# Attention values of a Macaron block: full 512-column matmuls against 256-column passes with 64-row key blocks

## The chip, the cores and the metric

The kernel runs on one core of one Trainium2 chip. The metric is the device time in microseconds (us) of one launch. All data are float32.

## The reference

```
x = x + 0.5 * ffn(layernorm(x));  x = x + attn(layernorm(x));  x = x + 0.5 * ffn(layernorm(x))
ffn:   base = x @ W_base.T + b_base
       plus, with weights w from a top-2 softmax router over 8 experts, 2 * sum_e w_e * (x @ A_e.T) @ B_e.T   (rank 16)
attn:  q = rope(x @ wq) (32 heads of 128), k = rope(x @ wk), v = x @ wv (8 heads of 128), S = 256
       allowed = (j <= i) & (j > i - 128)             # a causal window of 128 keys
       out = softmax(q k^T / sqrt(128), allowed) @ v;  return out @ wo
```

The input x is 4 sequences of 256 tokens, each of width 512.

## The kernel before

The tokens are handled in two halves `h` of two sequences each. A **group** `(h, g)` is one key head `g` with its 4 query heads, and a **unit** `(h, g, b)` is one group on one sequence `b` of the half: 16 groups, 32 units. Units go in order, two to a group (`b` = 0, then `b` = 1).

For each unit the loop at L708 writes this work, one unit ahead where it can: keys (L374) and value projections (L465, tile `pv`) for a later group; `normalize` (L524, GpSimd) of this unit's probabilities; the output products of the *previous* unit (`outputs`, L581, tile `y`), which wait in the queue `late`; where `b` is 0, the queries of the next group (L400); `transposes` (L533, L537, L542); `scores` of the next unit (L482 `sa`, L497 `sb`); `values` (L553 to L561) of this unit; and the exponentials of the next unit (L515, ScalarE). ScalarE and GpSimd keep the order in which the loop writes their work. The order on TensorE and VectorE is the scheduler's.

**Blocks of keys.** The 256 queries of a head are four blocks of 64. The first two need only keys 0 to 127. Each of the last two needs three key blocks of 64, but of the first and the last of the three a query uses complementary triangles only. `scores` therefore folds these two into one block (L502), so that the probabilities of every pair of blocks are 128 x 128. After the transposition, where rows are keys, `transposes` parts the folded block again: it multiplies once by the mask `old` and once by `new` (L542), which gives `p1 = [old_p, new_p]`. Each has the third query block in columns 0 to 255 (`e` = 0: 4 heads x 64 queries) and the fourth in columns 256 to 511 (`e` = 1). `old_p` is multiplied with the values of keys 0 to 127 (`va` in the diff), `new_p` with those of keys 128 to 255 (`vb`). In the third block, `new_p` is zero in rows 64 to 127; in the fourth, `old_p` is zero in rows 0 to 63.

**`values` before.** The bank `oa` takes one matmul of 512 columns: `p0`, the first two query blocks, with the values of keys 0 to 127. The bank `ob` takes two: `old_p` and `new_p`, added up. A float32 matmul is two weight loads and two passes in the profile, so this is 6 passes of 512 columns a unit. ScalarE copies each bank to the tile `oT` as it is finished: `oa` to the first 128 tokens, `ob` to the last 128.

**After `values`.** `outputs` multiplies `oT` with the output weights by a scheme with 7 products instead of 8. It needs four sums and differences of the quarters of `oT`, made on GpSimd (`sums_a`, L114; tile `oTs`). Their order is: first minus second 128 tokens of heads 0 and 1; for the last 128 tokens, heads 0 and 1 plus heads 2 and 3; then `s2`; then `s4`. The products come in the order 4, then 1 and 6, then 2 and 3, then 7 and 5. Product 4 and product 1 take quarters of `oT` as they are. Product 6 takes `s2`, which is the third GpSimd instruction.

All matmul banks (`mm_bank`) come from one pool of four PSUM banks.

Of the kernel before, what the change touches and what calls it, by code (L numbers as in the profile page):

```python
# [17 lines left out]
P = 128  # L18
# [4 lines left out]
G = NH // NKV  # L23
# [6 lines left out]
BLK = 64  # L30
# [7 lines left out]
def macaron_kernel(  # L38
# [15 lines left out]
    nc = tc.nc  # L54
# [5 lines left out]
    def mm_bank(name):  # L60
        return ps.tile([P, 512], F32, tag="mm", bufs=4, name=name)
# [466 lines left out]
    def transposes(h, g, b, pr):  # L528
        def turn(n0, name):
            pt = ps.tile([P, 2, G, BLK], F32, tag="s", bufs=4, name=f"{name}_{h}_{g}_{b}")  # L530
            for p in range(G // 2):
                for e in range(2):
                    nc.tensor.transpose(pt[:, e, 2 * p : 2 * p + 2, :], pr[:, n0 + 2 * p + e, :], ident)  # L533
            return pt

        p0 = sb.tile([P, 2, G, BLK], F32, tag="p0", bufs=1, name=f"p0_{h}_{g}_{b}")
        nc.scalar.copy(p0, turn(0, "t0"))  # L537
        pt = turn(G, "t1")
        parts = []
        for n, w in enumerate((old, new)):  # L540
            part = sb.tile([P, 2, G, BLK], F32, tag=f"p1{n}", bufs=1, name=f"p1{n}_{h}_{g}_{b}")
            nc.vector.tensor_tensor(  # L542
                part, pt, w.unsqueeze(2).to_broadcast([P, 2, G, BLK]), ALU.mult
            )
            parts.append(part)
        return p0, parts

    def values(h, g, b, p0, p1):
        oT = sb.tile([HD, G, S], F32, tag="oT", bufs=4, name=f"oT_{h}_{g}_{b}")
        v = vS[h, g - g % 2]  # L550
        cols = ts(g % 2, HD)
        for i, parts in enumerate(([p0], p1)):
            po = mm_bank(f"o{'ab'[i]}_{h}_{g}_{b}")  # L553
            for n, part in enumerate(parts):
                nc.tensor.matmul(  # L555
                    po, v[:, 2 * b + n, cols], part, start=(n == 0), stop=(n == len(parts) - 1)
                )
            nc.scalar.copy(  # L558
                oT[:, :, ts(i, P)].rearrange("p j (e q) -> p e j q", e=2),
                po.rearrange("p (e j q) -> p e j q", e=2, j=G),  # L560
            )  # L561
        return oT

# [144 lines left out]
    for u, (h, g, b) in enumerate(units):  # L708
        n = groups.index((h, g)) + 1
# [26 lines left out]
        p0, p1 = transposes(h, g, b, ahead[0])  # L736
# [5 lines left out]
        if left > 1:  # L742
            ahead = scores(*units[u + 1])
        oT = values(h, g, b, p0, p1)
        if left > 1:
            exponentials(*ahead)
# [67 lines left out]
```

## Time and profile before

| what | value |
|---|---|
| median of 3 runs | 792.85 us (792.47 to 793.61) |
| the profiled execution's own time | 793.98 us |
| its span, first to last instruction | 792.3 us |
| TensorE (PE) busy | 780.0 us, 98% of the span |
| share of PE in the chain that ended last | 96% |
| VectorE (DVE), ScalarE (ACT), GpSimd (POOL) busy | 61%, 28%, 57% |
| granted TensorE clock | 1.000 |

PE is the matmuls and PEld the weight loads, which have rows of their own. A matmul's row gives the time from its start to the end of its result; neighbours overlap, so the cost of one in a row of many is the distance from start to start, which the timeline gives. A merged line of the timeline (x8) stands for several instructions of one kind; the next line's start tells how long they held the engine. In brackets stands the time that the engine sat idle before a line, and what released it.

### The profile page before, as it was taken

To read this page: it belongs to the slowest core of one execution; us is meant where nothing else is said; L and a number is where in the kernel's file an instruction comes from. 1 tells how busy PE (TensorE), PEld (TensorE's weight loads), DVE (VectorE), ACT (ScalarE), POOL (GpSimd) and SP (SyncE) were. 2 spreads that over 40 slices of the span, in tenths; PEclk is the share of its full clock that TensorE was granted. 3 is DMA by queue.
4 is the path that set the end of the run, shared out by engine and by line. 5 is a ranking of instruction groups with operands and counts; after the bars stand their busy time and mean duration, and the time that the engine had idled before them with its cause. 6 is when DMAs were issued, how large, how long until landed. Compare 5 with 4: busy or idle time off the path is not lost.

```text
span 792.3 us, 10145 instructions
## 1 busy us (share of the span) xinstructions
PE 780.0 (98%) x3524; PEld 602.6 (76%) x3524; DVE 486.6 (61%) x1226; ACT 222.1 (28%) x766; POOL 451.4 (57%) x461
## 2 busy tenths in 40 slices
PE   6999999999999999999999999999999999999998
PEld 4557878787878888787878787878788787877654
DVE  4558563838474756659487728484757557574663
ACT  4342333222213140312222232213141412223331
POOL 5421775674747474757575665747474756653521
PEclk9999999999999999999999999999999999999999
DMA  8400221212021302112121212020303021100001
GB/s 294 158 1 19 76 67 53 93 54 67 8 99 41 106 14 91 57 53 67 54 95 53 67 54 88 23 95 9 106 14 101 20 58 49 54 1 26 1 27 54
DMA packets 33555, 48.90 MB, mean 62 GB/s; under 512 B 1248, under 2 KB 14304, under 8 KB 33504
## 3 DMA queue, kind: packets, MB, share of 16 engines
q1 hardware_dynamic: 33504, 48.26, 18.6%
q8 instruction: 28, 0.46, 0.2%
q14 instruction: 23, 0.19, 0.1%
HBM read 46.15 MB, written 2.10 MB: 61 GB/s over the span
## 4 chain that ended last, share of the span: by engine, by line
PE 96%; DMA 1%; DVE 1%; ACT 1%; SPq 0%; POOL 0%; issue 0%; DVEq 0%; ACTq 0%
PE q L400 24%; PE y L581 23%; PE pv L465 7%; PE ob L555 7%; PE pp_k L374 7%; PE po_f L330 6%; PE sb L497 5%; PE sa L482 4%; PE t L533 4%; PE oa L555 3%; PE pa_f L317 2%; PE po_f L342 1%; DMA x<-in_x_dram 1%; PE y L620 1%; PE pt_f L246 1%; ACT probs L515 0%
## 5 line engine op out<-in xcount | busy, mean ns | idle before, releaser
L369 POOL TENSOR_TENSOR qT<-ra_q,rb_q 128x512 f32<-128x512 f32 x64 | 81.4, 1272 | 154.9 <-DVE rb_q L365 154.9
L581 PE MATMUL y<-wo,oT 128*128 128x256 f32 x368 | 94.8, 379 | 0.0
L365 DVE TENSOR_TENSOR rb_q<-q,sin_sb 64x512 f32<-64x512 f32 x128 | 88.1, 688 | 1.7
L597 DVE TENSOR_TENSOR x<-y,x 128x256 f32<-128x256 f32 (+1 forms) x62 | 34.0, 548 | 83.0 <-PE y L581 82.9
L114 POOL TENSOR_TENSOR oTs<-oT 128x256 f32<-128x256 f32 x62 | 45.8, 738 | 59.7 <-ACT oT L558 57.2
L581 PEld LDWEIGHTS y<-wo,oT 128*128 128x128 f32 x368 | 69.8, 190 | 9.4
L537 ACT COPY p<-t 128x512 f32<-128x512 f32 x32 | 18.8, 586 | 203.1 <-PE t L533 203.1
L524 POOL TENSOR_TENSOR probs<-probs,sm 128x512 f32<-128x512 f32 x64 | 66.2, 1055 | 1.2 <-DVE sm L519 1.2
L581 PE MATMUL y<-wos,oTs 128*128 128x256 f32 x248 | 63.9, 380 | 0.6 <-POOL oTs L114 0.6
L465 PEld LDWEIGHTS pv<-wv,xa 128*128 128x128 f32 x256 | 48.6, 190 | 18.1 <-issue 12.9
L400 PE MATMUL q<-xa,wq 128*128 128x256 f32 x256 | 60.8, 379 | 0.0
L400 PE MATMUL q<-xs,wqs 128*128 128x256 f32 x256 | 60.6, 379 | 0.0
L400 PE MATMUL q<-xs,wq 128*128 128x256 f32 x256 | 60.5, 379 | 0.0
L555 PE MATMUL ob<-p,v 128*128 128x512 f32 x128 | 60.1, 592 | 0.0
L465 PE MATMUL pv<-wv,xa 128*128 128x256 f32 x256 | 60.0, 379 | 0.0
L330 PE MATMUL po_f<-wb_sb,xn_f 128*128 128x512 f32 x128 | 57.9, 594 | 0.0
L374 PE MATMUL pp_k<-xa,wk 128*128 128x512 f32 x128 | 57.5, 592 | 0.0
L590 DVE TENSOR_TENSOR z<-y,z 128x512 f32<-128x512 f32 x46 | 31.7, 690 | 40.2 <-PE y L581 40.2
L515 ACT ACTIVATE probs<-probs,nm 128x64 f32<-128x64 f32 (+1 forms) x128 | 46.3, 364 | 35.7 <-DVE nm L511 30.2
L400 PEld LDWEIGHTS q<-xa,wq 128*128 128x128 f32 x256 | 48.5, 190 | 6.9 <-issue 0.2
L400 PEld LDWEIGHTS q<-xs,wqs 128*128 128x128 f32 x256 | 48.6, 190 | 6.6
L581 PEld LDWEIGHTS y<-wos,oTs 128*128 128x128 f32 x248 | 46.9, 190 | 7.5 <-POOL oTs L114 1.0
(142 smaller groups left out, 1489.2 us busy)
## 6 DMA issues: line engine op xcount, KB each, us to landing
wq<-in_wq_dram SPq DMA_DIRECT2D x16, 1024.0 KB, 5.4
wo<-in_wo_dram SPq DMA_DIRECT2D x16, 1024.0 KB, 5.3
wk<-in_wk_dram SPq DMA_DIRECT2D x16, 256.0 KB, 2.7
wv<-in_wv_dram SPq DMA_DIRECT2D x8, 512.0 KB, 3.5
x<-in_x_dram SPq DMA_DIRECT2D x8, 256.0 KB, 7.2
out_dram<-x SPq DMA_DIRECT2D x8, 256.0 KB, 2.0
wb_sb<-in_w_base_dram SPq DMA_DIRECT2D x1, 1024.0 KB, 7.8
ar_sb<-in_w_ar_dram SPq DMA_DIRECT2D x1, 272.0 KB, 4.8
```

Source lines behind the costliest of these rows:

```text
L114: nc.gpsimd.tensor_tensor(dst, p, q, op)
L330: nc.tensor.matmul(po[i], x_of(i, c), wb_sb[:, c, :], start=(c == 0), stop=False)
L365: nc.vector.tensor_tensor(twice(b[o : o + half, :]), twice(src[i : i + half, :]), angle(sin_sb[o : o + half, :]), ALU.mult,)
L369: nc.gpsimd.tensor_tensor(dst, view(a), view(b), ALU.add)
L374: nc.tensor.matmul(pp, w[:, c, :], xa[h][:, c, :], start=(c == 0), stop=(c == KC - 1))
L400: nc.tensor.matmul(bank[:, ts(j, S)], w[:, c, ts(j, HD)], x[:, c, :], start=(new and j == 0 and c == 0), stop=(c == 1), skip_group_check=True,
L465: nc.tensor.matmul(pv[:, : 2 * HD], xa[h][:, c, ts(i, P)], weights["v", h, g][:, c, :], start=(c == 0), stop=(c == KC - 1),)
L497: nc.tensor.matmul(pb[:, ts(e, 3 * BLK)], q[:, 2 + e, 2 * p : 2 * p + 2, :], k[:, n - P : n + BLK], start=True, stop=True,)
L515: nc.scalar.activation(pr[:, n, :keys_of], src[:, :keys_of], AF.Exp, bias=nm[:, n : n + 1], scale=scale, accum_out=sm[:, n : n + 1],)
L524: nc.gpsimd.tensor_tensor(w, w, sm[:, n : n + G].unsqueeze(2).to_broadcast([P, G, P]), ALU.mult)
L555: nc.tensor.matmul(po, v[:, 2 * b + n, cols], part, start=(n == 0), stop=(n == len(parts) - 1))
L581: nc.tensor.matmul(py[:, ts(i, D // 2)], lhs[n - 1][:, c, :], weights["os", h, g][n - 1][:, c, :], start=(i == 0 and c == 0), stop=(c == 1 ...
```

## The change

Only `values` is changed. Two banks are open at once. The bank of index `e` holds, in columns 0 to 255, the first (`e` = 0) or second (`e` = 1) query block, and in columns 256 to 511 the third or fourth.

- Four matmuls of 128 rows and 256 columns: `p0` of each block with `va`, then `old_p` of the third block with `va` and `new_p` of the fourth with `vb`.
- Four matmuls of 64 rows and 128 columns for what is left: `new_p` of the third block in rows 0 to 63 into bank 0, and `old_p` of the fourth block in rows 64 to 127 into bank 1. Each is cut in two by columns, and the two row groups take turns.
- Then the two copies to `oT`. Each bank now holds 64 of every 128 tokens, so each copy writes to both halves of the tokens, and each of the quarters that `sums_a` reads comes from both copies.

```
         cols = ts(g % 2, HD)
-        for i, parts in enumerate(([p0], p1)):
-            po = mm_bank(f"o{'ab'[i]}_{h}_{g}_{b}")
-            for n, part in enumerate(parts):
+        old_p, new_p = p1
+        va, vb = (v[:, 2 * b + n, cols] for n in range(2))
+        banks = [mm_bank(f"o{n}_{h}_{g}_{b}").rearrange("p (e c) -> p e c", e=2) for n in "ab"]
+        def block(t, e):
+            return t[:, e, :, :].rearrange("p j q -> p (j q)")
+        for e in range(2):
+            nc.tensor.matmul(banks[e][:, 0, :], va, block(p0, e), start=True, stop=True)
+        nc.tensor.matmul(
+            banks[0][:, 1, :], va, block(old_p, 0), start=False, stop=False, skip_group_check=True
+        )
+        nc.tensor.matmul(
+            banks[1][:, 1, :], vb, block(new_p, 1), start=False, stop=False, skip_group_check=True
+        )
+        for c in range(2):
+            for bank, lhs, rhs in (
+                (banks[0], vb[:BLK], block(new_p, 0)[:BLK]), (banks[1], va[BLK:], block(old_p, 1)[BLK:]),
+            ):
                 nc.tensor.matmul(
-                    po, v[:, 2 * b + n, cols], part, start=(n == 0), stop=(n == len(parts) - 1)
+                    bank[:, 1, ts(c, P)], lhs, rhs[:, ts(c, P)], start=False, stop=True,
+                    skip_group_check=True,
                 )
+        for e in range(2):
             nc.scalar.copy(
-                oT[:, :, ts(i, P)].rearrange("p j (e q) -> p e j q", e=2),
-                po.rearrange("p (e j q) -> p e j q", e=2, j=G),
+                oT.rearrange("p j (i e q) -> p e i j q", i=2, e=2)[:, e],
+                banks[e].rearrange("p i (j q) -> p i j q", j=G),
             )
         return oT
```

## The prediction

> **What bounds the kernel now.** I read the page's busy shares and its chain first.
>
> ```profile
> span 792.3 us, 10145 instructions
> PE 780.0 (98%) x3524; PEld 602.6 (76%) x3524; DVE 486.6 (61%) x1226; ACT 222.1 (28%) x766; POOL 451.4 (57%) x461
> PE 96%; DMA 1%; DVE 1%; ACT 1%; SPq 0%; POOL 0%; issue 0%; DVEq 0%; ACTq 0%
> L581 PE MATMUL y<-wos,oTs 128*128 128x256 f32 x248 | 63.9, 380 | 0.6 <-POOL oTs L114 0.6
> ```
>
> TensorE is the bound: what its passes lose or gain moves the end, and so does any wait put before one of them. Other engines count only through such waits; the last line is one that hardly exists yet. Next the timeline around `values` in a unit with b = 0, for the price of a pass.
>
> ```profile
> 310.42 1.04 PE L533 MATMUL t<-ident,probs 128*128 128x128 f32 x8
> 311.29 1.89 PE L400 MATMUL q<-xs,wq 128*128 128x256 f32 x8
> 313.02 1.05 PE L482 MATMUL sa<-kT,qT 128*128 128x64 f32 x8
> 313.91 1.47 PE L497 MATMUL sb<-kT,qT 128*128 128x192 f32 x8
> 315.21 1.02 PE L555 MATMUL oa<-p,v 128*128 128x512 f32 x2
> 316.07 1.88 PE L555 MATMUL ob<-p,v 128*128 128x512 f32 x4
> 317.79 3.60 PE L374 MATMUL pp_k<-xa,wk 128*128 128x512 f32 x8
> 317.99 0.59 ACT L558 COPY oT<-ob 128x512 f32<-128x512 f32 x1 [1.13 <-PE ob L555]
> ```
>
> Start to start: 8 passes of 128 columns take 311.29 - 310.42 = 0.87 us (0.109 each), 8 of 256 take 1.73 (0.216), 6 of 512 take 317.79 - 315.21 = 2.58 (0.43). `sa` (half 64, half 128 columns) takes 0.89 for 8, or 0.111 each, where streaming alone would give 0.082 by the rate of `t`; its 8 weight loads set that pace, so one load per 0.111 is the floor for loads that follow one another. The page's mean of a pass (592, 380, 273 ns) exceeds its distance by 0.162 to 0.164: the time from the last column to the end of the result. The copy of `ob` starts 0.20 after the next matmul does.
>
> Last, the timeline behind `values` in a unit with b = 1, to see who needs `oT` and when.
>
> ```profile
> 290.57 1.88 PE L555 MATMUL ob<-p,v 128*128 128x512 f32 x4
> 292.29 1.89 PE L465 MATMUL pv<-wv,xa 128*128 128x256 f32 x8
> 292.49 0.59 ACT L558 COPY oT<-ob 128x512 f32<-128x512 f32 x1 [1.13 <-PE ob L555]
> 292.97 0.35 ACT L515 ACTIVATE probs<-probs,nm 128x64 f32<-128x64 f32 x1
> 293.15 0.73 POOL L114 TENSOR_TENSOR oTs<-oT 128x256 f32<-128x256 f32 x1 [3.29 <-ACT oT L558]
> 293.96 0.72 POOL L114 TENSOR_TENSOR oT<-oT 128x256 f32<-128x256 f32 x1
> 294.01 1.03 PE L581 MATMUL y<-wos,oT 128*128 128x256 f32 x4
> 294.76 0.73 POOL L114 TENSOR_TENSOR oTs<-oT 128x256 f32<-128x256 f32 x1
> 294.88 1.03 PE L581 MATMUL y<-wo,oT 128*128 128x256 f32 x4
> 295.55 0.60 PEld L581 LDWEIGHTS y<-wos,oTs 128*128 128x128 f32 x3
> 295.74 0.38 PE L581 MATMUL y<-wos,oTs 128*128 128x256 f32 x1
> ```
>
> GpSimd sits idle until the second copy ends (293.08), then makes three sums; the third ends at 295.49, and the weight load of product 6, which reads it, starts at 295.55, exactly when its turn comes (products 4, 1 and 6 start 0.87 and 0.86 apart: no gap yet). So this chain, copy, three sums, load, has no slack. I followed it through all units: 14 of the 16 with b = 1 look like this (0.04 to 0.06 us from sum to load); in most with b = 0 the load comes 1.98 us after the sum, because a key projection lies between. The two left, at the end, have 3.1 us, and no such product.
>
> **The change part by part.** *Passes.* Of 6 x 0.43 = 2.58 us a unit, 8 passes of 256 columns remain as 8 x 0.216 = 1.73. The rest becomes 8 passes of 64 rows and 128 columns. No row shows a matmul with fewer than 128 rows, so I bound it. One after another they cost 8 x 0.109 = 0.87 by `t`, or 0.89 at the loads' pace of `sa`: 2.60 to 2.62 in all, 0.02 to 0.04 dearer than now. If passes on different rows run at once, the two passes of one matmul still share their rows, so only the second pass of one lies beside the first of the next: 5 slots, 0.55, and 2.28 in all, 0.30 cheaper. Perfect pairs would be 4 slots, 0.44, and 0.41 cheaper. Over 32 units: +0.6 to +1.3, -9.6, or -13.1 us. Among these I take 5 slots.
>
> *Switching.* The array goes from 128 rows to 64 and back in each unit. No row shows a switch. It can't be a gain, as the passes around it already follow each other without a gap. Its price lies between nothing and an array that first empties (0.164) and only then takes a load (0.190, the page's mean of a load): 0.354. Twice 32 times: 0, 10.5 (emptying alone), or 22.7 us. I take emptying alone, as loads run ahead of matmuls in every row above.
>
> The Trainium skill speaks against the change here: "TensorEngine Tiling (Array Packing)", Key Properties, states that changing the tiling mode drains the engine, while changing only the tile within a mode does not. No run here shows it yet; by that rule the middle price holds and eats the overlap. The skill's "TensorE: Matmul & The Clock Gate", Part 3, The mechanism, states that a weight load overlaps running matmuls only where the row groups differ; the 128-row passes above, whose 0.190 loads hide wholly beside 0.216 passes on the same rows, disagree, so I don't charge for it.
>
> *Copies.* Today `oa` is copied while `ob` is computed, and the last copy ends 0.20 + 0.59 = 0.79 after the last pass's turn ends. Afterwards bank 0 is complete only one matmul before bank 1. If its two passes take 0.22, the first copy starts at -0.02, the second 0.59 later, ending at 1.16: 0.37 later than now. With overlap bank 0 ends only 0.11 before: 0.48 later. If consecutive ScalarE instructions overlap as copy and exponential do (292.49 to 292.97, 0.48), each is 0.11 less. Bounds 0.26 and 0.48; I take 0.37, nearest to plain copies. Queued behind on ScalarE are the exponentials; the probabilities they feed are transposed at 310.42 only, so that hides. GpSimd waits, and product 6 with it, since nothing stands between: 14 x 0.37 = 5.2 us (3.6 to 6.7). A gap on leaving the 64-row passes delays TensorE itself by as much, so it covers part: with emptying alone, 14 x (0.37 - 0.16) = 2.9.
>
> *The rest at nothing.* Units with b = 0 have 1.98 us of cover; uncovered they would cost as much again. Both banks are taken at once, but the older matmul banks are read long before, and banks freed up to 1.7 us later are next needed after a key or value projection (3.4 or 1.7). `new_p` is ready at 313.5 for a use at about 316.5. In the last unit the first output product needs both copies instead of the early one: up to 1.4 us once if nothing fills it; I take 0.7.
>
> *Sum.* -9.6 + 10.5 + 2.9 + 0.7 = +4.5 us on the profiled 793.98 (span 792.3 and 1.7 around it): 798.5. The median of the runs shown is 1.1 lower, 792.85, so I state **797.4**.
>
> **The rivals.** *Overlap with a free switch.* The array takes 64-row passes without emptying: -9.6 + 14 x 0.42 (5.9) + 0.7 = -3.0, hence 789.8; with perfect pairs and the shortest copies -13.1 + 3.6 = -9.5, hence 783.4. For it: the array keeps loads and passes in flight together everywhere in this profile. Against: half of the gain goes to the copies.
>
> *The 64-row passes don't do what they are meant to*: they follow one another, switching is free. +1.0 + 5.2 + 0.7 = +6.9, hence 799.8. For it: the loads of `sa` set their own pace of 0.111 although the matmuls are shorter, and eight loads stay eight loads.
>
> *Emptying that nothing pays for.* Serial passes and emptying at both ends: 1.0 + 10.5 + 2.9 + 0.7 = +15.1, hence 808.0; overlapped, but each switch with its load exposed (0.354, which covers nearly all of the copies' wait): -9.6 + 22.7 + 0.2 + 0.7 = +14.0, hence 806.9; serial and exposed +24.6, hence 817.5. From 0.15 us a switch on, overlap gains nothing; this case needs more than twice that, or no overlap.
>
> **How the numbers follow.** About 0.2% (1.6 us) is what a measurement can tell from no change. Overlap paid back by emptying, my forecast: 0.30, at 797.4. Overlap with a free switch: 0.27. Serial and free: 0.13. Costly switches: 0.24, and 0.06 for the worst of them. Forecast and first rival border on each other: a switch of 0.06 us gives no change, which gets 0.05, taken from both. Faster 0.26, same 0.05, slower 0.69. The likeliest case alone spans 794 to 802 (copies 0.26 to 0.48, switch 0.12 to 0.22). Both signs counted, 786 to 812 leaves out the best of the second case and the serial, exposed one.
>
> **What would show it.** In the profile after: the distance from the first to the last 64-row pass against 0.55 and 0.87; from the last 256-column pass to the first 64-row one, and from the last of these to the next 128-row pass, beyond a pass's own distance, against 0, 0.16 and 0.35; the second copy ending about 1.16 instead of 0.79 after that; and an idle time of some 3 to 6 us before product 6 put down to GpSimd's sums, in place of 0.6. I am wrong if the two row groups' passes start together with no gap around them, if the second copy starts earlier than I say, or if the scheduler puts other matmuls between the 64-row ones, which would multiply the switches.

## The result and the profile after

The changed kernel takes 796.96 us (median of 4 runs, 796.26 to 797.12) against 793.23 us for the kernel before in the same comparison: ratio 1.0046, 95% interval 1.0031 to 1.0061, some 3.7 us slower. The forecast was 797.4.

The page of the changed kernel, with the same lines as before; its line numbers are shifted (L601 is the L581 of before, L573 the 64-row matmuls, L578 the copies, L617 and L640 the former L597 and L620):

```profile
span 795.1 us, 10785 instructions
PE 783.1 (98%) x3844; PEld 628.2 (79%) x3844; DVE 487.6 (61%) x1226; ACT 218.6 (27%) x766; POOL 451.6 (57%) x461
PE 95%; DVE 2%; DMA 1%; ACT 0%; SPq 0%; POOL 0%; issue 0%; ACTq 0%; DVEq 0%
L601 PE MATMUL y<-wos,oTs 128*128 128x256 f32 x248 | 65.2, 385 | 0.4 <-POOL oTs L114 0.4
L601 PEld LDWEIGHTS y<-wos,oTs 128*128 128x128 f32 x248 | 45.8, 190 | 10.7 <-POOL oTs L114 5.0
```

TensorE is as full as before. The wait that I had announced before product 6 hardly shows in the matmuls' row (0.4 us); it stands in the row of their weight loads, 5.0 us put down to GpSimd. In the page of before that row has 1.0:

```profile
L581 PEld LDWEIGHTS y<-wos,oTs 128*128 128x128 f32 x248 | 46.9, 190 | 7.5 <-POOL oTs L114 1.0
```

A look at the matmuls alone would have missed it. A late load is not yet a loss of the same size, though; the timeline below gives the loss.

The timeline of the changed kernel in the same unit as before (b = 1), first the passes:

```profile
290.41 0.59 PE L566 MATMUL ob<-p,v 128*128 128x256 f32 x2
290.94 0.18 PEld L573 LDWEIGHTS oa<-p,v 64*128 64x128 f32 x1 [0.33 <-issue]
290.94 0.37 PE L573 MATMUL oa<-p,v 64*128 64x128 f32 x1
290.94 0.18 PEld L573 LDWEIGHTS ob<-p,v 64*128 64x128 f32 x1
290.95 0.37 PE L573 MATMUL ob<-p,v 64*128 64x128 f32 x1
291.15 0.27 PE L573 MATMUL oa<-p,v 64*128 64x128 f32 x1
291.16 0.27 PE L573 MATMUL ob<-p,v 64*128 64x128 f32 x1
291.26 0.27 PE L573 MATMUL oa<-p,v 64*128 64x128 f32 x1
291.27 0.27 PE L573 MATMUL ob<-p,v 64*128 64x128 f32 x1
291.38 0.27 PE L573 MATMUL oa<-p,v 64*128 64x128 f32 x1
291.38 0.27 PE L573 MATMUL ob<-p,v 64*128 64x128 f32 x1
291.58 1.59 PEld L465 LDWEIGHTS pv<-wv,xa 128*128 128x128 f32 x8
291.58 1.99 PE L465 MATMUL pv<-wv,xa 128*128 128x256 f32 x8
293.42 1.03 PE L601 MATMUL y<-wos,oT 128*128 128x256 f32 x4
```

The eight passes of 64 rows are four perfect pairs: each `oa` pass starts with an `ob` pass beside it, and inside the mode pair follows pair after 0.11 us. So they take four slots (a slot is the time that one pass of 128 columns holds the array). The switches stand at both ends. The last 256-column pass gives up its place at 290.41 + 2 x 0.216 = 290.84, and the first pair starts at 290.94 (0.10 idle); the second pair comes after 0.21 instead of 0.11, since the first weight load was not made ahead (0.10). The last slot ends at 291.49, `pv` starts at 291.58 (0.09), and its eight passes take 1.84 instead of 1.73 until 293.42, again for a load that did not run ahead (0.11). One visit to the 64-row mode, in and out again, so costs 0.40 us beside its passes. From the start of `values` to the first output product it is 4.30 us, 289.12 to 293.42; before, `values` started with this line, and the first output product at 294.01, also 4.30. Overlap and switches cancel.

```profile
289.71 1.02 PE L555 MATMUL oa<-p,v 128*128 128x512 f32 x2
```

Then the copies and product 6 in the same timeline:

```profile
291.68 0.58 ACT L578 COPY oT<-oa 128x512 f32<-128x512 f32 x1 [4.36 <-PE ob L573]
292.17 0.59 ACT L578 COPY oT<-ob 128x512 f32<-128x512 f32 x1
292.83 0.72 POOL L114 TENSOR_TENSOR oTs<-oT 128x256 f32<-128x256 f32 x1 [3.57 <-ACT oT L578]
294.28 1.03 PE L601 MATMUL y<-wo,oT 128*128 128x256 f32 x4
294.44 0.73 POOL L114 TENSOR_TENSOR oTs<-oT 128x256 f32<-128x256 f32 x1
295.22 0.73 PEld L601 LDWEIGHTS y<-wos,oTs 128*128 128x128 f32 x4 [0.32 <-POOL oTs L114]
295.22 1.13 PE L601 MATMUL y<-wos,oTs 128*128 128x256 f32 x4
296.19 1.03 PE L601 MATMUL y<-wo,oT 128*128 128x256 f32 x4
```

Both copies now stand one behind the other after the last pass. The second ends at 292.76, 0.66 us before product 4 starts; before it was 0.93. GpSimd's third sum ends at 295.17, and only then comes the load of product 6. Product 1 starts at 294.28 and the one after product 6 at 296.19: 1.91 instead of 1.73, so 0.18 us are lost. I compared the start of every unit's transposes (L533) in the two traces: the changed kernel loses this 0.18 once a group, 13 times, and 0.09 at the 14th, from -1.29 us at the first unit to +1.09 at the unit with b = 1 of the last group but one: 2.4 us. The -1.29 arose ahead of any changed instruction; other runs below start at -0.4 to -1.4, and the medians don't rest on it.

The rest is lost at the end. The last unit, in the timeline of the changed kernel:

```profile
757.69 0.71 PE L573 MATMUL oa<-p,v 64*128 64x128 f32 x4
758.33 0.70 PE L562 MATMUL ob<-p,v 128*128 128x256 f32 x2
758.87 0.59 PE L566 MATMUL ob<-p,v 128*128 128x256 f32 x2
759.39 0.71 PE L573 MATMUL ob<-p,v 64*128 64x128 f32 x4
760.78 1.98 PE L640 MATMUL y<-wo,oT 128*128 128x512 f32 x4 [0.68 <-ACT oT L578]
```

Here the scheduler took the two row groups apart: two visits, nothing beside anything, and then 0.68 us until the second copy lets the first output product start. In the kernel before, that product followed the last pass of `values` without a gap:

```profile
756.30 1.88 PE L555 MATMUL ob<-p,v 128*128 128x512 f32 x4
758.02 2.74 PE L620 MATMUL y<-wo,oT 128*128 128x512 f32 x6
```

From the start of this unit's `values` to the last matmul group the trace falls behind from 1.28 to 2.84 us: 1.6.

### The profile page after: what moved, and what is told of

Read it like the earlier page. It is cut to its first block, busy times and chain, and to the rows that moved or that the text cites. A ratio compares the mean times of both kernels' runs of the same rounds, so it can differ in the third digit from the quotient of the medians.

```text
span 795.1 us, 10785 instructions
## 1 busy us (share of the span) xinstructions
PE 783.1 (98%) x3844; PEld 628.2 (79%) x3844; DVE 487.6 (61%) x1226; ACT 218.6 (27%) x766; POOL 451.6 (57%) x461
## 4 chain that ended last, share of the span: by engine, by line
PE 95%; DVE 2%; DMA 1%; ACT 0%; SPq 0%; POOL 0%; issue 0%; ACTq 0%; DVEq 0%
PE q L400 24%; PE y L601 23%; PE pp_k L374 7%; PE pv L465 7%; PE po_f L330 6%; PE sb L497 5%; PE sa L482 3%; PE t L533 3%; PE oa L573 2%; PE ob L566 2%; PE ob L562 2%; PE po_f L342 2%; PE oa L563 2%; PE oa L562 2%; PE pa_f L317 2%; DMA x<-in_x_dram 1%
## 5 line engine op out<-in xcount | busy, mean ns | idle before, releaser
L601 PE MATMUL y<-wo,oT 128*128 128x256 f32 x368 | 94.4, 379 | 0.0
L617 DVE TENSOR_TENSOR x<-y,x 128x256 f32<-128x256 f32 (+1 forms) x62 | 34.0, 548 | 83.3 <-PE y L601 83.2
L601 PEld LDWEIGHTS y<-wo,oT 128*128 128x128 f32 x368 | 69.9, 190 | 9.5
L601 PE MATMUL y<-wos,oTs 128*128 128x256 f32 x248 | 65.2, 385 | 0.4 <-POOL oTs L114 0.4
L578 ACT COPY oT<-oa 128x512 f32<-128x512 f32 x32 | 18.7, 585 | 163.9 <-PE ob L573 161.0
L374 PE MATMUL pp_k<-xa,wk 128*128 128x512 f32 x128 | 59.1, 604 | 0.0
L601 PEld LDWEIGHTS y<-wos,oTs 128*128 128x128 f32 x248 | 45.8, 190 | 10.7 <-POOL oTs L114 5.0
```

Source lines behind the costliest of these rows:

```text
L374: nc.tensor.matmul(pp, w[:, c, :], xa[h][:, c, :], start=(c == 0), stop=(c == KC - 1))
L601: nc.tensor.matmul(py[:, ts(i, D // 2)], lhs[n - 1][:, c, :], weights["os", h, g][n - 1][:, c, :], start=(i == 0 and c == 0), stop=(c == 1 ...
L617: nc.vector.tensor_tensor(dst, py[:, : len(which) * D // 2], dst, ALU.add)
```

## The experiments

The theory behind the first set: overlap is worth some 0.43 us a unit, a visit to the 64-row mode costs as much, and the loss is the late copies and the end. The rival: the switches are dearer than the overlap, and the copies harmless.

**Rows of zeros instead of 64-row matmuls.**

```
-  (banks[0], vb[:BLK], block(new_p, 0)[:BLK]), (banks[1], va[BLK:], block(old_p, 1)[BLK:]),
+  (banks[0], vb, block(new_p, 0)), (banks[1], va, block(old_p, 1)),
```

> The 64-row matmuls are replaced by matmuls of all 128 rows on the same 128 columns (the added rows hold zeros); banks, order and copies stay as in the changed kernel. Theory (the overlap of the two row groups, worth some 0.43 us a unit, is paid back by entering and leaving the 64-row mode, some 0.42 a unit; the late copies cost on their own): TensorE's time a unit stays within 0.03 us of the kernel before, and as no gap on leaving covers part of the copies' delay, product 6 comes 0.25 to 0.3 late in 14 units (3.5 to 4.2 us) and the end loses about 1: 797.5 to 799.5 us. Rival (the copies are harmless, the switches make the loss): 793 to 795.

797.96 us, ratio 1.0061 (1.0048 to 1.0074). With no switch and no overlap the kernel is about as slow as with both. TensorE's time around `values` grows by 0.04 us (eight passes take 0.89), and the trace falls behind by 0.26 a group, of which 0.18 before product 6 and 0.08 in the passes. The 0.18 is less than the 0.25 to 0.3 that I expected. The rival, which put the loss in the switches, is out.

**The same passes, visited twice.**

```
-  p0 | old_p, new_p | 64 rows, c = 0 and 1
+  p0 | 64 rows, c = 0 | old_p, new_p | 64 rows, c = 1
```

> The 64-row matmuls of the first 128 columns go before the two full matmuls of old_p and new_p, those of the last 128 columns behind them: the same passes, but twice as many switches. Theory (0.42 us for going into the mode and out again): 32 x 0.42 = 13.4 us more than the changed kernel, 808 to 812. Rival (only the idle time visible at the switches counts, about 0.19, the rest of the 0.42 belongs to the passes): 802 to 804.

810.53 us, ratio 1.0218 (1.0204 to 1.0232): 13.6 us above the changed kernel, 0.42 for each of the 32 added visits. The same unit in the timeline of this kernel:

```profile
292.98 0.59 PE L562 MATMUL oa<-p,v 128*128 128x256 f32 x2
295.84 2.00 PE L465 MATMUL pv<-wv,xa 128*128 128x256 f32 x8
297.67 1.03 PE L609 MATMUL y<-wos,oT 128*128 128x256 f32 x4
```

From the start of `values` to the first output product it is 4.69 us instead of 4.30, and the starts of the transposes fall behind those of the changed kernel by 0.40 a unit through the loop; the rest of the 13.6 falls at the two ends of the trace. So a visit in the loop costs 0.40. The price belongs to going in and out, and the part hidden in the first loads counts as much as the visible gaps.

**The 64-row matmuls in the middle.**

```
-  p0 | old_p, new_p | 64 rows
+  p0 | 64 rows | old_p, new_p
```

> The same instructions as in the changed kernel, with the 64-row matmuls moved between the two matmuls of p0 and the two full matmuls of old_p and new_p. Bank 0 is now complete 0.43 us before bank 1, so the second copy ends some 0.06 us later than in the kernel before instead of 0.2 to 0.3. Theory (late copies make the loss, overlap and switches cancel): the wait of product 6 falls from about 0.18 a unit to 0.06 or less, 793.3 to 795 us. Rival (the switches are dearer than the overlap is worth): as the changed kernel, 796.5 to 797.5.

795.68 us, ratio 1.0029 (1.0018 to 1.0040): more than I expected, less than the rival. The loop did what was expected. In the unit shown above (timeline of this kernel),

```profile
291.58 0.59 ACT L578 COPY oT<-oa 128x512 f32<-128x512 f32 x1 [4.13 <-PE oa L571]
292.06 0.59 ACT L578 COPY oT<-ob 128x512 f32<-128x512 f32 x1
293.54 1.03 PE L601 MATMUL y<-wos,oT 128*128 128x256 f32 x4
294.40 1.03 PE L601 MATMUL y<-wo,oT 128*128 128x256 f32 x4
295.26 1.03 PE L601 MATMUL y<-wos,oTs 128*128 128x256 f32 x4
```

the second copy ends 0.89 us before product 4, and products 4, 1 and 6 start 0.86 apart: the wait is gone. Over the loop this kernel even gains 0.005 us a unit on the kernel before. Its loss is all at the end, where it goes from 0.46 us ahead of the kernel before to 1.68 behind: there its last unit takes three visits. The prediction had allowed 0.7 for the end.

**The last unit with the values of before**, once in the kernel just shown, once in the changed kernel.

```
-  oT = values(h, g, b, p0, p1)
+  oT = (values if left > 1 else values_whole)(h, g, b, p0, p1)     # values_whole: the function before
```

> As e3_middle, but the last unit uses the values of the kernel before, whose early copy the first output product of the end waits for. Theory (what e3_middle has left, 2.5 us, is the end, where the trace shows 2.1 us; in the loop overlap and switches cancel): 793 to 794 us, no difference from the kernel before. Rival (the loop or the start costs it): 795 to 796.

> As the changed kernel, but the last unit uses the values of the kernel before. The loop then still has the wait of product 6, some 0.18 us in 14 units. Theory (of the changed kernel's 3.7 us, about 1.5 are lost at the end and 2.5 in the loop): 795.2 to 795.9 us. Rival (all of it comes from the loop): 796.5 to 797.5.

With the 64-row matmuls in the middle: 793.07 us against 793.02, ratio 1.0000 (0.9991 to 1.0009). With nothing late, overlap and switches leave no difference. In the changed kernel: 795.24, ratio 1.0032 (1.0019 to 1.0044). So the order inside `values`, by which the copies come late, costs 2.2 us (795.24 - 793.07), and the end 1.5 to 1.7: 796.96 - 795.24 is 1.7, from two comparisons, and 1.5 if each is taken against its own time of the kernel before. The trace has 1.6.

**No turns, and no cut by columns.** The prediction had assumed that passes start in program order. These two ask what the pairs depend on.

```
 first:   oa c=0, oa c=1, ob c=0, ob c=1      instead of   oa c=0, ob c=0, oa c=1, ob c=1
 second:  oa, ob, each of 64 rows and 256 columns
```

> As the changed kernel, but the two row groups don't take turns in program order: first both 64-row matmuls into bank 0 (rows 0 to 63), then both into bank 1 (rows 64 to 127). In the trace of the changed kernel the second row group's first pass starts with the first group's first pass, although its own matmul stands two passes later in program order. Theory (each row group works off its own passes, ahead of the other): still 4 slots of 0.11, 796.5 to 797.5 us. Rival (passes start in program order, as the prediction assumed): 7 slots instead of 4, 0.33 us a unit more, 806 to 808.

> As the changed kernel, but each 64-row matmul takes all its 256 columns at once: two matmuls of 64 rows instead of four, half as many weight loads. Theory (the two row groups run beside each other, whatever their order): 2 slots of 0.216 as against 4 of 0.11, the same 0.43 us, 796 to 797.5. Rival (the cut into columns is what lets the row groups overlap, in program order): 3 slots, 0.22 us a unit more, 803 to 805.

Without turns 797.67 us, ratio 1.0061 (1.0046 to 1.0077); 7 slots would have brought 806 or more. It lies 0.2 us above the expected window, and its interval overlaps with that of the changed kernel. Unsplit 796.42, ratio 1.0043 (1.0028 to 1.0059). The timeline without turns:

```profile
291.08 0.37 PE L573 MATMUL oa<-p,v 64*128 64x128 f32 x1
291.09 0.37 PE L573 MATMUL ob<-p,v 64*128 64x128 f32 x1
291.29 0.27 PE L573 MATMUL oa<-p,v 64*128 64x128 f32 x1
291.31 0.27 PE L573 MATMUL ob<-p,v 64*128 64x128 f32 x1
```

The first `ob` pass starts 0.01 us after the first `oa` pass, though three `oa` passes stand between them in program order. The scheduler kept that order: in the trace of the changed kernel the last `ob` matmul raises the semaphore that the copies wait for by exactly one in 31 of 32 units, right after an `oa` matmul that raises it too; here it raises it by more than one in all 32, as it must with another `ob` matmul just ahead that raises nothing. Neither the turns nor the cut earn anything that these runs can tell.

**One visit for two units.** If a visit has a price of its own, sharing it should pay. `values_pair` computes both units of a group after the second one's scores: the full matmuls of the first unit, all 64-row matmuls, the full matmuls of the second. The output products move one unit later.

```
+  whole_blocks(one); half_blocks(one); copies of one
+  half_blocks(two);  whole_blocks(two); copies of two
```

> The values of both units of a group are computed together, after the second one's scores, so that one visit to the 64-row mode serves two units (15 groups; the last group goes unit by unit). The 64-row passes stand so that the last bank's copy ends 0.79 us after the last pass, as in the kernel before. Output products of a unit move one unit later, and the second set of weight sums and a weight load with them. Theory (a switch has a price of its own, 0.42 in and out): a group takes 8 x 0.43 + 8 x 0.11 + 0.42 = 4.75 us instead of 5.16, 15 x 0.41 = 6.2 us less than before, 786 to 789; up to 0.5 us a group can be lost if the probabilities of the second unit are now late, as 2.6 us of TensorE's work no longer stands before them: at worst 794. Rival (the price goes with the passes, not with the switch): no gain, 793 to 797.

823.5 us, ratio 1.0382 (1.0368 to 1.0396), far off. The pair itself costs what was worked out, 4.74 us from its first pass to the next projection (timeline of this kernel; the first unit's probabilities lie in the buffer of its `oT`):

```profile
292.48 0.59 PE L577 MATMUL oa<-oT,v 128*128 128x256 f32 x2
297.22 1.89 PE L465 MATMUL pv<-wv,xa 128*128 128x256 f32 x8
```

What I had not followed was GpSimd, whose sums of the output weights I had moved into the second unit:

```profile
298.43 1.27 POOL L114 TENSOR_TENSOR wqs<-wq,wqs 128x512 f32<-128x512 f32 x1
299.66 0.73 POOL L114 TENSOR_TENSOR oTs<-oT 128x256 f32<-128x256 f32 x1
301.27 0.72 POOL L114 TENSOR_TENSOR oTs<-oT 128x256 f32<-128x256 f32 x1
302.05 1.13 PE L637 MATMUL y<-wos,oTs 128*128 128x256 f32 x4 [1.21 <-POOL oTs L114]
```

It had been at weight sums without a pause since 289.04 and came to `oT` late; product 6 waited (26.7 us in the loads' row). Two waits of 2.4 us near the start were each followed by some 3.4 us at a granted clock of 0.50, which adds an estimated 3.4 us.

**Two buffers for the weight sums**, so that GpSimd makes them in the first unit again.

```
-  if b == 1: sum_o_weights(h, g); load_o(next group)        # tag "wos", bufs=1
+  if b == 0: sum_o_weights(h, g)                            # tag "wos", bufs=2
+  if b == 1: load_o(next group)
```

> As e7_pairs, but with two buffers for the sums of the output weights, so that GpSimd makes them in the first unit of a group again, where it has idle time; the two units of the last group use the values of the kernel before. (Room for it comes from one buffer less of the tiles oT and xc.) Theory (e7_pairs lost its gain to GpSimd alone, which came to the sums of oT some 2 us late in each group; a visit to the 64-row mode shared by two units saves 0.41 a group): 15 x 0.41 = 6.2 us less than the kernel before, 786 to 789. Rival (the moved output products and the smaller number of buffers cost as much elsewhere): 793 to 800.

796.46 us, ratio 1.0042 (1.0029 to 1.0054): the waits for GpSimd's sums are gone and 27 us with them, but the gain of 6.2 did not come. The trace gains 0.26 us a group in the steady part, not 0.41; product 2 waits 0.15 for a matmul bank that VectorE frees late. And it loses in the first group, where the moved products leave TensorE with nothing until the probabilities of the second unit are there (waits of `t`):

```profile
113.06 0.66 PE L533 MATMUL t<-ident,probs 128*128 128x128 f32 x4 [2.38 <-POOL probs L524]
114.06 0.66 PE L533 MATMUL t<-ident,probs 128*128 128x128 f32 x4 [0.34 <-POOL probs L524]
115.65 2.77 PE L497 MATMUL sb<-kT,qT 128*128 128x192 f32 x8
```

The wait costs more than its 2.7 us. After it the granted clock is 0.81, 0.50 and 0.84 in the windows 114 to 116, 116 to 118 and 118 to 120, some 1.7 us lost by these three numbers; the eight passes of `sb` take 2.77 us instead of 1.47.

**Pairs from the second group on.**

```
+  alone = end or n == 1        # first and last group: unit by unit, values of the kernel before
```

> As e8_pairs_two_sums, but the first group goes unit by unit with the values of the kernel before, and pairs begin with the second group. In e8_pairs_two_sums TensorE waited 2.7 us for the probabilities of the second unit, because the first group's output products, moved one unit later, had left their place empty; later groups gained 0.26 each. Theory (the visit shared by two units is a gain once that hole is filled): 13 groups at 0.26, less 0.7 between the halves: 790 to 791.5 us. Rival (the hole moves to the second group with the transition): 794 to 796.

791.09 us against 793.05, ratio 0.9976 (0.9967 to 0.9984): faster than both kernels, and inside the expected 790 to 791.5. With the wait the drop of the clock is gone too (1.00 in all windows from 100 to 130). The overlap is a gain once a visit serves two units. The trace still gains 0.26 a group and not 0.41, for the 0.15 before product 2 has stayed. No run has this order of work with the full-width passes of before; that the gain comes from the pair is read from the trace, where a pair takes 4.74 us and two units took 5.16.

## Why the prediction was right

The forecast was 797.4 with the mechanism "overlap paid back by emptying, the loss from the copies". Time and mechanism held: overlap and switches cancel, and late copies and the end make the loss. That the time came out within 0.5 us is in part luck, as four terms were off and their errors nearly cancel. By its steps:

*Passes.* I took 5 slots, because I let passes start in program order and the two passes of one matmul share their rows. Measured: 4 slots, the perfect pairs that I kept as the lower bound. The gain is therefore about 0.41 us a unit, 13.1 in all, not 9.6. The run without turns shows the assumption itself to be wrong. Of my signs of being wrong half of one came: the passes start together, but with gaps around them; and in the last unit the scheduler did put other matmuls between the 64-row ones.

*Switching.* I took an emptying at each end, 0.33 a visit, 10.5 in all. Measured: 0.40 in the trace and in the loop of the run with two visits, 12.8 in all. The term is larger and made up otherwise: half of it is idle time, half a first load that did not run ahead. The errors of passes and switches, 3.5 and 2.3 us, have opposite signs, and that is the luck. That overlap and switching cancel each other is not: it was forecast, and the run that keeps both in the loop and loses nothing shows it (ratio 1.0000).

*The rule on modes.* The Trainium skill, "TensorEngine Tiling (Array Packing)", Key Properties, states that a change of tiling mode drains the engine. The runs agree that a change costs and a pass inside the mode doesn't: 0.40 more for a second visit with the same passes. They don't show that the whole array empties: the two idle gaps of 0.10 and 0.09 are shorter than the 0.16 that I had put on emptying, and the first 64-row pass starts at 290.94, before the last result of the pass ahead is out (291.00, a modelled end).

*Copies.* I said the second copy would end 1.16 us after the last pass, 0.37 later than before, less 0.16 covered by the exit: 0.21 in 14 units, 2.9 us. Measured: 1.27 (291.49 to 292.76), so 0.48 later. Both banks are complete together, and the first copy starts 0.19 after the last slot instead of 0.02 before it; that the copies overlap by 0.09 on ScalarE (the first ends at 292.26, the second starts at 292.17) takes part of this back. The exit covers 0.20, which leaves GpSimd's sums some 0.27 late, and the load of product 6 has 0.08 to spare, as it may come 0.11 instead of 0.19 ahead of its pass before the pass is late. What is left is the 0.18 a group, 2.4 us in the trace and 2.2 between two runs.

*The end.* I took 0.7 with a bound of 1.4; it was 1.6. I had counted the wait for the second copy (0.68, as it came) but not that the scheduler would part the two row groups there and pay two visits without an overlap.

*The sum.* For 31 units, 12.7 gained by the passes and 12.4 lost to visits; 2.4 lost to the copies, 1.6 in the last unit: 3.7 us, as measured.

*The rivals.* "Overlap with a free switch" had the passes right in its variant with perfect pairs, but not the switch. "The passes don't do what they are meant to" named 799.8; the run with full rows, which has no overlap and no switch, took 797.96, as its copies cost less than I had put. The dear switches did not come.

## What to carry to other kernels

A mode of the array that costs something to enter and to leave is paid per visit, so it pays only where enough work is done in one visit: here 0.40 us a visit against 0.41 us saved is nothing, and two units to a visit is a gain. When an edit changes which part of a result is finished when, look for the reader with no slack: here a copy 0.27 us later cost more than all that was done to the matmuls. And a step moved to another place in the loop takes its engine's queue with it: the pairs first lost 27 us to sums on GpSimd that had only been moved one unit on, and then a wait in the first group ate the gain until that group was left as it was.

## What the runs showed of the hardware that I had not expected

- Passes on different row groups don't start in program order: a row group's first pass started 0.01 us after the other's first, with three of the other's passes between them in the program. The Trainium skill, "TensorE: Matmul & The Clock Gate", Part 3, The mechanism, states that matmuls keep program order in start and end; here the measurement decides, for the starts of float32 passes on two row groups (the ends in a trace are modelled).
- Weight loads of the two row groups also go side by side: eight loads and eight passes fit into four slots of 0.11 us, where full-width loads that follow one another took 0.111 each (both first loads start at 290.94).
- Inside the 64-row mode a load runs ahead as usual; across a switch it does not, which costs 0.10 to 0.11 us on each side beside the idle gap.
- In the run with two buffers the granted clock fell to 0.50 after TensorE had waited 2.38 and 0.34 us, and was back at 1.00 by 120 us. Not every wait did this: in the first run with pairs, one of 2.6 us at 388.5 left the clock at 1.00.
